# Values first, sums of exps by ones-products, and products of constants in long waits: a change to the start and the first image of a two-layer attention kernel

## The chip, the core and the metric

The kernel runs on one core of one Trainium2 chip. The metric is device time in microseconds (us) of one execution; the profile's times are microseconds from the first instruction, in one profiled execution. The engines are TensorE (PE, matrix products into PSUM), VectorE (DVE), ScalarE (ACT), GpSimd (POOL) and SyncE (SP, which here only starts transfers). Each engine works through its own instructions in the order in which the program wrote them.

## The reference

Input x has 8 images of 256 channels by 32 x 32 positions. Everything is float32. Layer 0, for each image:

```python
q = einsum('bchw,oc->bohw', x, q_w)            # x is group-normalised first
kv = einsum('bchw,oc->bohw', x, kv_w)          # k_map, v_map: 256 channels each
# pooled(t): for sides 32, 16, 11, 5: p = average-pooled t; p = p + depthwise 3x3 convolution of p
ks_ = _layernorm(pooled(k_map).transpose(0, 2, 1), norm_w, norm_b)   # 1024+256+121+25 = 1426 tokens
vs_ = _layernorm(pooled(v_map).transpose(0, 2, 1), norm_w, norm_b)
attn = softmax(einsum('bhqd,bhkd->bhqk', q_g, k) * SCALE)            # 8 heads of 32
out_att = einsum('bhqk,bhkd->bhqd', attn, v)
# a mixing matrix per head from a global token, a projection, and x is added
```

Layer 1 is self-attention over the 1024 positions of each image (one head of 256) and a sum over eight experts of three dense layers, weighted by a gate. The change touches layer 0 alone, its first image most of all.

## The kernel before

**The main loop** (lines 2012 to 2067). Layer 0's attention is cut into units. A unit is one image b, one half c of the heads (four heads), and one half of the queries (512); four units make an image. Keys come in 12 chunks of 128 (the last one smaller, and done for a whole image in one tail step). A step of a unit makes the scores of four heads (`scores`, line 1558: four products into the four-bank PSUM tile `sc`), takes their exp on ACT into a tile `pt` (128 x 2048, six buffers), and, one step later, multiplies them by the values into `pv` (`values`, line 1568). `sc` has one buffer, so the next scores wait for the exp before.

**The sum of the exps.** Two `pt` tiles at a time are added by a transfer that accumulates in memory (`add`, line 1613, on POOL's queue: the trace's pt<-pt). That leaves six pairs a unit. In `sums` (line 1620) DVE adds pairs 1 to 5 to pair 0, in two halves each (the rows pt<-pt,pt), and at the end four products with a 128 x 32 matrix of ones sum pair 0 over the partitions, each into its own 32 columns of the array. `normalise` (line 1639) then divides.

**The background and the planner.** All else (image b+1's keys and values, layer 1 of the images before, weights) is written as Python generators, called threads. `Flow` (line 661) is a planner that runs while the program is built. It keeps a modelled time for each engine and for when each tile is ready (`note`, `cost`, `transfer`), and each thread says what it waits for (`yield pe(tile, tag="sm")`: PE needs this tile and a free small PSUM bank). `step` lets background threads that are ready write their instructions between two steps of the loop, lower rank first, within a budget of PE time; `finish` runs threads until a condition holds. So the order on every engine is fixed when the program is built, by modelled times. Nothing is reordered on the chip by real times.

**PSUM.** Small products share two banks with the tag `sm`, and a third, `sx`, that `small()` (line 944) takes when it is free sooner. In the main loop a plain 128-wide product may be split into four products of 32 columns (`narrow`).

**The start** (before the first step). `prepare(0)` (line 1427) normalises x. `pool_levels` (line 1386) pools x to sides 11 and 5, on POOL and DVE, through a work tile with the tag `pool` that has one buffer; `halve` (line 1137) pools a projected map to side 16 on POOL, through the same tag. `first_maps` (line 1216) projects the four maps of image 0: m = 0, 1 are the two channel halves of the keys, m = 2, 3 those of the values. It writes the large side as two slices of 512 columns, at column 0 and 512, and the small sides as one slice (`HW`). The order is: keys' large slices, values' large slices, then all small ones. ACT copies each slice out and, for values, also writes the centre tap into `acc`. The queries (line 1477, four products of 512 columns for image 0) are a thread of their own with rank 3, next to it.

Keys' large side is convolved on PE with diagonal matrices (`first_keys`, line 1270, in two halves of the image). The values' large side, and all small sides, are convolved on DVE, eight shifted multiply-adds a map and side (`taps`, line 1295; the trace's acc<-map,vec,acc, kn<-ptail and v<-ptail). `first_taps` (line 1309) writes them in this order: values' large side, then the small sides of keys and of values, and it waits until all large slices of all maps are planned. Then `key_tokens` and `value_tokens` transpose to tokens (tiles kt and vt), DVE takes their statistics (tst, tmean, tshift), ACT normalises. They go in three groups of four chunks, so steps 0 to 3, 4 to 7 and 8 to 11 of a unit each need their group.

The next image's `prepare` begins with the load of its x once the four queries of image 0 have been planned (line 1430).

Of the kernel before, what the change touches and what calls it, by code (L numbers as in the profile page):

```python
# [16 lines left out]
P = 128  # L17
C = 256
HW = 1024
HEADS = 8  # L20
DH = 32
# [3 lines left out]
NKC = 12  # L25
# [12 lines left out]
OWN = {"pt", "p1"}  # L38
BUFS = {"sm": 2, "sx": 1}
AHEAD3 = 3  # L40
PACE2 = 8.0
NBOUND = 64
NSTAGED = 64
# [617 lines left out]
class Flow:  # L661
# [4 lines left out]
    class Engine:  # L666
# [3 lines left out]
        def __getattr__(self, op):  # L670
            fn = getattr(self.eng, op)

            def call(*args, **kwargs):
                ins = fn(*args, **kwargs)  # L674
                self.flow.note(self.name, op, ins, args, kwargs)
                return ins

            if op != "matmul":
                return call

            def product(out, lhsT, rhs, **kwargs):
                if not self.flow.narrow(lhsT, rhs):
                    return call(out, lhsT=lhsT, rhs=rhs, **kwargs)
                for j in range(0, P, DH):
                    call(out[j : j + DH], lhsT=lhsT[:, j : j + DH], rhs=rhs, **kwargs)

            return product

    def __init__(self, tc, kit):
        nc = tc.nc  # L690
        self.tc, self.kit = tc, kit
        self.now = dict.fromkeys(("PE", "DVE", "ACT", "POOL", "SP"), 0.0)
        self.last = {}
        self.ready, self.read, self.writer, self.reader, self.slots, self.open = {}, {}, {}, {}, {}, set()
        self.pe = self.Engine(self, "PE", nc.tensor)
        self.ve = self.Engine(self, "DVE", nc.vector)
        self.act = self.Engine(self, "ACT", nc.scalar)
        self.pool = self.Engine(self, "POOL", nc.gpsimd)
        self.sp = self.Engine(self, "SP", nc.sync)
        self.threads = []  # L700
        self.held = set()
        self.cut = {}
        self.also = {}
        self.tiled = None
        self.columns = False
        self.left, self.served = [0.0, 0.0], 0.0
        self.credit, self.port = [0.0, 0.0], 0.0
# [120 lines left out]
    def transfer(self, queue, at, work):  # L828

        span = max(0.0, at - self.served)  # L830
        self.served = max(self.served, at)
        mine, other = queue == "POOL", queue != "POOL"
        left = self.left
        both = 2 * min(left)
        done = min(span, both) / 2
        for i in range(2):
            left[i] = max(0.0, left[i] - done - max(0.0, span - both))
        left[mine] += work
        return 2.2 + left[mine] + min(left[mine], left[other]) + self.served - at

    @staticmethod
    def key(a):
# [85 lines left out]
def attention(tc, kit, f, outer, ended, nb, consts, x, t1, t2, hn, bounds, vecs, q_t, kv_t, proj_t, gqk_t, wqk, wqkv, vecs1, w1_d, w1c, gate_d, wrc, vecs2, bnvec, w2_d, h2d, between, pre, held):  # L928
# [6 lines left out]
    with ExitStack() as ctx:  # L935
# [197 lines left out]
        def source(xp, s0, w):  # L1133
            xi, xl = xp
            return xi[:, :, s0 : s0 + w] if s0 < HW else xl[:, :, s0 - OFFS[2] : s0 - OFFS[2] + w]

        def halve(p, small_p, c, acc):

            yield pool(p[:, :HW])
            pm = p[:, :HW].rearrange("p (h w) -> p h w", h=32)  # L1140
            t2 = T(work, [P, 32, 16], "pool")
            f.pool.tensor_tensor(t2, pm[:, :, 0::2], pm[:, :, 1::2], ALU.add)
            yield pool(t2)
            l2 = small_p.rearrange("p (h w) -> p h w", h=16)
            f.pool.tensor_tensor(l2, t2[:, 0::2, :], t2[:, 1::2, :], ALU.add)
            yield act(small_p)
            f.act.activation(
                acc[:, HW : OFFS[2]],
                small_p,
                AF.Identity,  # L1150
                bias=db(c, 1),
                scale=mid[:, c * 4 + 1 : c * 4 + 2],
            )
            halved.append(acc)
# [61 lines left out]
        def first_maps(xp):  # L1216


            for m in range(4):
                if m < 2:  # L1220
                    p = T(work, [P, 4, 512], "pt", bufs=6).rearrange("p j q -> p (j q)")
                    acc = T(l1, [P, NK], "v") if m else T(work, [P, NK], "kn", bufs=3)
                else:
                    p = pmaps[m - 2]
                    acc = T(work, [P, NK], "acc", bufs=3)
                for t in (p, acc):
                    if t is not p or m < 2:
                        f.split(t, 512, HW)
                first[m] = p, acc
            for m, s0 in [(m, s0) for g in (0, 2) for s0 in (0, 512) for m in (g, g + 1)] + [(m, HW) for m in range(4)]:  # L1230
                if s0 == HW:
                    yield until(lambda: pooled)
                    s0 = OFFS[2]
                w = min(512, NK - s0)
                c = m % 2
                p, acc = first[m]
                src = source(xp, s0, w)
                yield pe(src, tag="sm")
                ps = small()
                for k in range(2):  # L1240
                    f.pe.matmul(
                        ps[:, :w],
                        lhsT=kvw[:, k, m * P : (m + 1) * P],
                        rhs=src[:, k, :],
                        start=k == 0,
                        stop=k == 1,
                    )
                small_levels = s0 > HW and m < 2
                f.act.activation(
                    ptail[:, m, s0 - HW : s0 - HW + w] if small_levels else p[:, s0 : s0 + w], ps[:, :w], AF.Copy  # L1250
                )
                for s, n in enumerate(SIDES):
                    a, z = max(OFFS[s], s0), min(OFFS[s] + n * n, s0 + w)
                    if a < z and (m >= 2 or s):
                        f.act.activation(
                            acc[:, a:z],
                            ps[:, a - s0 : z - s0],
                            AF.Identity,
                            bias=db(c, s),
                            scale=mid[:, c * 4 + s : c * 4 + s + 1],  # L1260
                        )
                if s0 == 512:
                    f.spawn(halve(p, ptail[:, m, :256] if m < 2 else p[:, HW : OFFS[2]], c, acc), 0)
                if (m, s0) == (3, 512):
                    large.append("maps")
                    f.spawn(first_keys(0), 1)
                    f.spawn(first_keys(1), 5)
            whole.append("maps")

# [38 lines left out]

        def first_taps():
            for m in (2, 3):  # L1310
                yield until(lambda: "maps" in large)
                yield from taps(m - 2, 0, *first[m])
                large.append(("values", m))
                read[0] += 1
# [71 lines left out]
        def pool_levels(xi, xl):  # L1386
# [7 lines left out]
            for k in range(2):  # L1394
                one, l3 = img[:, k], level(2)[:, k]

                yield pool(xi)
                t3 = T(work, [P, 32, 11], "pool")
                f.pool.tensor_tensor(t3, one[:, :, 0::3], one[:, :, 1::3], ALU.add)
                yield pool(t3)  # L1400
# [5 lines left out]
                f.pool.tensor_tensor(l3[:, 0:10, :], l3[:, 0:10, :], t3[:, 2::3, :], ALU.add)  # L1406
                yield pool(t3)
                f.pool.tensor_tensor(l3[:, 1:11, :], l3[:, 1:11, :], t3[:, 2::3, :], ALU.add)
                flat = xl[:, k, : OFFS[3] - OFFS[2]]
                f.pool.tensor_tensor(flat, flat, con[:, K_S11 : K_S11 + 121], ALU.mult)  # L1410

            t5 = T(work, [P, 2, 32, 5], "pool")
            ends = [(i * 32 // 5, -(-(i + 1) * 32 // 5)) for i in range(5)]
            for i, (a, e) in enumerate(ends):
# [7 lines left out]
                )  # L1422
            flat = xl[:, :, OFFS[3] - OFFS[2] :]
            f.ve.tensor_tensor(flat, flat, con[:, None, K_S5 : K_S5 + 25].to_broadcast([P, 2, 25]), ALU.mult)
            pooled.append(True)

        def prepare(b):
# [38 lines left out]
            xp = xi, xl  # L1466
            if b == 0:
                todo.extend([None] * 4)
                f.spawn(queries(b, xi), 3)
                yield from first_maps(xp)  # L1470
            else:
                yield from maps(xp)
# [4 lines left out]
        def queries(b, xi):  # L1477

            for c in range(2):
                if b == 0:  # L1480
                    qs[b, c] = T(work, [P, HW], "q", bufs=2)
                for half in range(2):
                    sl = slice(half * 512, half * 512 + 512)
                    q = T(work, [P, 512], "pool") if b else qs[b, c][:, sl]
                    yield pe(xi, q, tag="sm")
                    ps = small()
# [8 lines left out]
                    f.act.activation(q, ps, AF.Copy, scale=vec[:, V_NW + c : V_NW + c + 1])  # L1495
                    if b:
                        f.sp.dma_start(hn[b][:, c, sl], q)
                    else:
                        asked.append((c, half))

# [118 lines left out]

        def sums(n, pairs):  # L1620

            for i in range(1, NKC // 2):
                yield until(lambda: len(pairs) > i)
                for j in range(0, 4, 2):
# [383 lines left out]
        f.spawn(chain(mix(), weights1(), outputs()), 5)  # L2008
        f.spawn(layer1(), 6)
        aside = f.spawn(experts_ahead(), 8)  # L2010
        f.columns = True
        order = [*range(8), NKC - 1, *range(8, NKC - 1)]
        steps = [
            (b, c, half, kc)
# [9 lines left out]
        for i in range(len(steps) + 1):  # L2024
# [40 lines left out]
                    f.act.activation(atts[b1, c1][:, sl1], pv, AF.Copy)  # L2065
            if i < len(steps):
                f.step((PACE, PACE1))
        f.columns = False
        f.finish(lambda: projected[0] == nb)
        f.finish(lambda: aside[1] is None)  # L2070
        f.also.clear()
# [713 lines left out]
```

## Time and profile before

| what | value |
|---|---|
| median of 3 runs | 3241.08 us (3239.82 to 3246.97) |
| the profiled execution's own time | 3241.31 us |
| its span, first to last instruction | 3238.0 us |
| mean granted TensorE clock | 0.983 of full |
| PE busy | 3052.4 us (94%) |
| DVE busy | 2388.8 us (74%) |
| ACT busy | 1631.2 us (50%) |
| POOL busy | 1224.7 us (38%) |
| DVE additions of exps, 128 x 1024 | 320 instructions, 391.7 us, mean 1269 ns |
| exps on ACT, 128 x 2048 | 352 full ones, 660.8 us, mean 1877 ns |
| first exp of the attention | at 80.1 us |
| first exps of units 2, 3, 4 | at 155.3, 204.1, 251.7 us |
| first exp of image 1 | at 295.5 us |

A row of the time-ordered view reads: start, duration of the merged group, engine, line, operation, output<-inputs with sizes, count, and in brackets how long the engine had been idle before and what ended that. All instructions that go through the planner have its one line, L674, so groups are told apart by their tiles. A float32 product shows as two instructions in the trace, so four products are "x8". A row of a stage table gives the stretch, its length, the busy time and count of PE, PE's weight loads, DVE, ACT and POOL, the granted clock, and the share and rate of transfers. In the slices, a digit is a tenth of busy time, and PEclk is the clock that PE was granted.

### The profile page before, as it was taken

To read this page: it belongs to the slowest core of one execution; us is meant where nothing else is said; L and a number is where in the kernel's file an instruction comes from. 1 tells how busy PE (TensorE), PEld (TensorE's weight loads), DVE (VectorE), ACT (ScalarE), POOL (GpSimd) and SP (SyncE) were. 2 spreads that over 40 slices of the span, in tenths; PEclk is the share of its full clock that TensorE was granted. 3 is DMA by queue.
4 is the path that set the end of the run, shared out by engine and by line. 5 is a ranking of instruction groups with operands and counts; after the bars stand their busy time and mean duration, and the time that the engine had idled before them with its cause. 6 is when DMAs were issued, how large, how long until landed. Compare 5 with 4: busy or idle time off the path is not lost.

```text
span 3238.0 us, 57063 instructions
## 1 busy us (share of the span) xinstructions
PE 3052.4 (94%) x22924; PEld 1774.1 (55%) x22924; DVE 2388.8 (74%) x4234; ACT 1631.2 (50%) x2168; POOL 1224.7 (38%) x1309
## 2 busy tenths in 40 slices
PE   8778899899999989989999999999999999999998
PEld 4222234334334333323433357777888888888887
DVE  6786778887988887888654435346878788777776
ACT  4566565566666566566655532334333333444443
POOL 3311413314332232231121121006755566776676
PEclk9899899999999999999999999999999999999999
DMA  1377646655666666656676673124444452000000
GB/s 54 75 163 163 131 98 147 138 135 107 146 143 132 153 130 123 149 121 119 135 190 127 151 220 127 72 91 163 144 152 146 146 173 73 20 20 33 20 14 21
DMA packets 118433, 377.68 MB, mean 117 GB/s; under 512 B 14720, under 2 KB 40648, under 8 KB 94928
## 3 DMA queue, kind: packets, MB, share of 16 engines
q0 software_dynamic: 28608, 179.85, 28.7%
q1 hardware_dynamic: 86048, 192.11, 17.5%
q8 instruction: 183, 3.00, 0.4%
q10 hardware_dynamic: 3504, 1.99, 0.2%
q14 instruction: 90, 0.74, 0.1%
HBM read 120.86 MB, written 87.60 MB: 64 GB/s over the span
## 4 chain that ended last, share of the span: by engine, by line
PE 46%; DVE 3%; issue 2%; DMA 1%; POOL 1%; ACT 1%; DVEq 0%; POOLq 0%; ACTq 0%
PE bank L674 21%; PE y L674 10%; PE sm L674 9%; PE sc L674 2%; PE pv L674 2%; PE sx L674 2%; DVE h L674 1%; DMA pt<-pt 1%; DVE u L674 1%; DVE c L674 1%; ACT pt L674 1%; POOL t L674 0%; DVE t L674 0%; POOL rstd L674 0%; DVE pt L674 0%
## 5 line engine op out<-in xcount | busy, mean ns | idle before, releaser
L674 ACT ACTIVATE pt<-sc 128x2048 f32<-128x2048 f32 x352 | 660.8, 1877 | 322.8 <-PE sc L674 262.9
L674 DVE TENSOR_TENSOR pt<-pt,pt 128x1024 f32<-128x1024 f32 x320 | 391.7, 1269 | 267.6 <-DMA pt<-pt 234.3
L674 DVE SCALAR_TENSOR_TENSOR acc<-map,vec,acc 128x961 f32<-128x961 f32 (+3 forms) x960 | 562.3, 594 | 34.6 <-ACT acc L674 9.3
L674 PE MATMUL sc<-q,kn 32*128 32x512 f32 (+1 forms) x3072 | 426.2, 663 | 101.7 <-ACT pt L674 97.8
L674 PE MATMUL pv<-pt,vt 128*32 128x512 f32 x2816 | 385.9, 621 | 3.6 <-ACT vt L674 3.6
L674 POOL TENSOR_TENSOR rstd<-rstd,mhalf 128x4 f32<-128x4 f32 (+2 forms) x88 | 105.4, 1199 | 719.6 <-DVE rstd L674 586.9
L674 ACT ACTIVATE h<-h,bnvec 128x512 f32<-128x512 f32 x440 | 332.8, 805 | 59.7 <-DVE h L674 50.6
L674 ACT ACTIVATE p1c<-bank 128x256 f32<-128x256 f32 x220 | 84.1, 382 | 549.9 <-PE bank L674 543.7
L674 POOL DMA_DIRECT2D pt<-pt x160 | 146.4, 919 | 435.1 <-ACT pt L674 374.8
L674 DVE TENSOR_TENSOR h<-p1c,bank 128x512 f32<-128x512 f32 x220 | 149.8, 681 | 201.9 <-PE bank L674 194.2
L674 PEld LDWEIGHTS sc<-q,kn 32*128 32x128 f32 (+1 forms) x3072 | 115.1, 181 | 294.1 <-ACT pt L674 188.2
L674 POOL TENSOR_TENSOR tm<-h,tm 128x256 f32<-128x256 f32 x202 | 233.9, 1158 | 15.8
L674 DVE TENSOR_TENSOR h<-u,bank 128x256 f32<-128x256 f32 (+1 forms) x440 | 223.9, 550 | 7.6
L674 PEld LDWEIGHTS pv<-pt,vt 128*32 128x32 f32 x2816 | 56.2, 109 | 281.1 <-issue 261.6
L674 POOL TENSOR_TENSOR tm<-h 128x512 f32<-128x512 f32 x101 | 128.5, 1273 | 195.9 <-ACT h L674 189.5
L674 DVE TENSOR_TENSOR h<-h,gate 128x1024 f32<-128x1024 f32 x128 | 199.4, 1558 | 0.5 <-ACT h L674 0.5
L674 PE MATMUL sm<-y,t 128*32 128x256 f32 (+1 forms) x2432 | 198.2, 379 | 1.1 <-DVE res L674 1.0
L674 PE MATMUL y<-t,s3e 128*128 128x256 f32 x768 | 187.0, 379 | 1.8 <-POOL t L674 1.7
L674 PE MATMUL sm<-p,v 128*32 128x256 f32 (+1 forms) x2064 | 179.5, 385 | 3.9 <-DVE turn L674 3.9
L674 PE MATMUL bank<-t,s1e 128*128 128x256 f32 x714 | 173.8, 379 | 0.2 <-DVE h L674 0.2
L674 POOL TENSOR_TENSOR t<-h 128x512 f32<-128x512 f32 x104 | 132.6, 1275 | 106.7 <-DVE h L674 85.8
L674 POOL TENSOR_TENSOR t<-h,t 128x256 f32<-128x256 f32 x208 | 163.9, 788 | 16.3
(368 smaller groups left out, 5422.3 us busy)
## 6 DMA issues: line engine op xcount, KB each, us to landing
pt<-pt POOLq DMA_DIRECT2D x160, 1024.0 KB, 7.8
h<-h SPq DMA_DIRECT2D x138, 512.0 KB
xi<-in_x_dram SPq DMA_DIRECT2D x16, 512.0 KB
t<-t SPq DMA_DIRECT2D x8, 1024.0 KB
res<-t SPq DMA_DIRECT2D x32, 256.0 KB
t<-res SPq DMA_DIRECT2D x32, 256.0 KB
hn<-res SPq DMA_DIRECT2D x32, 256.0 KB
hn<-hn SPq DMA_DIRECT2D x16, 512.0 KB
```

The source lines that it names most:

```text
L674: ins = fn(*args, **kwargs)
```

## The change

1. **Order of the start.** `first_maps` projects the values' large slices first (map 2, then map 3), then the keys' large slices, then the small slices of all four. `first_taps` waits for each value map by itself. The queries of image 0 become a thread after the last large key slice, beside the first keys' convolution. The users of the one-buffer `pool` tile exclude each other in the plan (`hold`).
2. **Sums of the first four units.** For these, which are image 0, `sums` no longer adds on DVE. It takes bank `sx` at its first pair and sums all six pairs with products of ones, accumulating in PSUM, each pair's buffer being given back after its products. It begins once the unit before has been normalised.
3. **Products of constants.** In the main loop, when the planner sees that a product's operands or its output bank will be ready 1.8 us or more after PE is free, and a small bank is free, it writes products of ones by constants (128 x 128 by 128 x 256) into that bank until the modelled wait is 1.3 us or less. Their results are read by nobody.

```diff
+SUMMED = 4
...
             def product(out, lhsT, rhs, **kwargs):
+                self.flow.warm(out, lhsT, rhs)
                 if not self.flow.narrow(lhsT, rhs):
...
+    def warm(self, out, *srcs):
+
+        if self.keep is None or self.free("sm") > self.now["PE"]:
+            return
+        at = max(self.ready.get(n, 0.0) for a in srcs for n in self.keys(a) if self.writer.get(n) != "PE")
+        for o in self.keys(out):
+            at = max(at, self.read.get(o, 0.0), self.ready.get(o, 0.0) * (self.writer.get(o) != "PE"))
+        if at - self.now["PE"] < 1.8:
+            return
+        bank, self.keep = self.keep, None
+        t = bank()
+        self.open.discard(t.name)
+        while at - self.now["PE"] > 1.3:
+            self.pe.matmul(t[:, :C], lhsT=self.kit.ones, rhs=self.kit.con[:, :C], start=True, stop=True)
+        self.keep = bank
...
+        pooling = []
+
+        def hold():
+
+            yield until(lambda: not pooling)
+            pooling.append(True)
+
         def halve(p, small_p, c, acc):
 
+            yield from hold()
             yield pool(p[:, :HW])
...
-            for m, s0 in [(m, s0) for g in (0, 2) for s0 in (0, 512) for m in (g, g + 1)] + [(m, HW) for m in range(4)]:
+            for m, s0 in [(m, s0) for m in (2, 3) for s0 in (0, 512)] + [
+                (m, s0) for s0 in (0, 512, HW) for m in (range(2) if s0 < HW else range(4))
+            ]:
...
-                if (m, s0) == (3, 512):
-                    large.append("maps")
+                if s0 == 512:
+                    large.append(("map", m))
+                if (m, s0) == (1, 512):
                     f.spawn(first_keys(0), 1)
+                    f.spawn(queries(0, xp[0]), 3)
                     f.spawn(first_keys(1), 5)
...
         def first_taps():
             for m in (2, 3):
-                yield until(lambda: "maps" in large)
+                yield until(lambda: ("map", m) in large)
...
-                f.spawn(queries(b, xi), 3)
                 yield from first_maps(xp)
...
+            if n < SUMMED:
+                yield until(lambda: normalised[0] == n)
+                total = None
+                for i in range(NKC // 2):
+                    yield until(lambda: len(pairs) > i)
+                    yield pe(pairs[i], tag=None if i else "sx")
+                    if i == 0:
+                        total = T(psum, [P, 512], "sx")
+                    for j in range(4):
+                        f.pe.matmul(
+                            total[DH * j : DH * j + DH, :],
+                            lhsT=kit.ones[:, :DH],
+                            rhs=pairs[i][:, j, :],
+                            start=i == 0,
+                            stop=i == NKC // 2 - 1,
+                        )
+                    f.drop(pairs[i])
+                return total
...
-        f.columns = True
+        f.columns, f.keep = True, small
...
-        f.columns = False
+        f.columns, f.keep = False, None
```

`hold` and `pooling.clear()` also stand around each use of the `pool` tile in `pool_levels` and, for later images, in `queries`.

More of the change, by code (lines that the diff above doesn't have):

```diff
@@ L700, in __init__ @@
         self.threads = []
+        self.keep = None
         self.held = set()
@@ L1145, in halve @@
             f.pool.tensor_tensor(l2, t2[:, 0::2, :], t2[:, 1::2, :], ALU.add)
+            pooling.clear()
             yield act(small_p)
@@ L1397, in pool_levels @@
                 yield pool(xi)
+                yield from hold()
                 t3 = T(work, [P, 32, 11], "pool")
@@ L1408, in pool_levels @@
                 f.pool.tensor_tensor(l3[:, 1:11, :], l3[:, 1:11, :], t3[:, 2::3, :], ALU.add)
+                pooling.clear()
                 flat = xl[:, k, : OFFS[3] - OFFS[2]]
                 f.pool.tensor_tensor(flat, flat, con[:, K_S11 : K_S11 + 121], ALU.mult)
+            yield from hold()
             t5 = T(work, [P, 2, 32, 5], "pool")
@@ L1424, in pool_levels @@
             f.ve.tensor_tensor(flat, flat, con[:, None, K_S5 : K_S5 + 25].to_broadcast([P, 2, 25]), ALU.mult)
+            pooling.clear()
             pooled.append(True)
@@ L1483, in queries @@
                     sl = slice(half * 512, half * 512 + 512)
+                    if b:
+                        yield from hold()
                     q = T(work, [P, 512], "pool") if b else qs[b, c][:, sl]
@@ L1497, in queries @@
                         f.sp.dma_start(hn[b][:, c, sl], q)
+                        pooling.clear()
                     else:
```

## The prediction

> **What bounds the kernel now.** I read the page's slices first, then busy time by stage, then each engine in order of time.
>
> ```profile
> PE   8778899899999989989999999999999999999998
> DVE  6786778887988887888654435346878788777776
> PEclk9899899999999999999999999999999999999999
> ```
>
> ```profile
> 76.78:153.76 76.98, 56.34 (x440) 24.12 (x440) 59.39 (x179) 45.16 (x61) 23.26 (x26) 0.83 0.33 71
> 153.76:202.93 49.17, 40.34 (x372) 12.21 (x368) 43.05 (x60) 29.03 (x31) 10.77 (x11) 0.90 0.68 148
> 202.93:249.35 46.42, 37.47 (x341) 13.04 (x337) 38.82 (x83) 35.23 (x43) 11.36 (x14) 1.00 0.72 158
> 249.35:294.29 44.94, 37.36 (x309) 10.69 (x305) 37.89 (x73) 26.82 (x24) 7.00 (x9) 0.96 0.74 180
> 294.29:457.00 162.71, 138.84 (x1280) 47.94 (x1280) 119.90 (x215) 105.98 (x126) 49.75 (x57) 0.95 0.62 128
> 457.00:1000.00 543.00, 508.21 (x5260) 205.96 (x5260) 454.11 (x890) 335.41 (x416) 165.14 (x182) 0.98 0.60 133
> ```
>
> The slices show a TensorE (PE) bound with a weak first eighth. The stage rows (PE, weight loads, DVE, ACT, POOL, granted clock) are, from the second line of numbers on, unit 1 to unit 4 of image 0 (one unit is 11 score steps of four heads and 512 queries), then image 1 to about its third unit, then the middle. PE idles 20.6 us in unit 1, 25.4 us in units 2 to 4 (140.5 - 115.2), 23.9 us in the next row, but only 34.8 us in the 543 us after that. So PE work is the bound from about 460 us on, and what comes before is waiting. A start that comes earlier is kept to the end, because the later work is then done in the same order, only sooner; PE work that is added counts in full unless it falls into idle time.
>
> Who is waited for in unit 1 is read in order of time:
>
> ```profile
> 35.93 19.27 DVE L674 SCALAR_TENSOR_TENSOR acc<-map,vec,acc 128x961 f32<-128x961 f32 x14 [9.27 <-ACT acc L674]
> ...
> 112.19 1.39 DVE L674 BATCH_NORM_STATS2 tst<-kt 128x6 f32<-128x256 f32 x4
> 113.51 2.33 DVE L674 TENSOR_TENSOR pt<-pt,pt 128x1024 f32<-128x1024 f32 x2
> 117.01 1.94 PE L674 MATMUL sx<-p,diag 128*32 128x256 f32 x16 [7.13 <-issue]
> ...
> 146.42 1.94 PE L674 MATMUL pv<-pt,vt 128*32 128x512 f32 x8 [3.55 <-ACT vt L674]
> ```
>
> ```profile
> 86.75 2.09 PE L674 MATMUL sc<-q,kn 32*128 32x512 f32 x8 [2.55 <-ACT pt L674]
> ...
> 90.84 1.14 PE L674 MATMUL sc<-q,kn 32*128 32x512 f32 x8
> ...
> 171.67 1.04 PE L674 MATMUL sm<-pt,con 128*32 128x512 f32 x8
> ```
>
> ```profile
> PE sc L674 <- ACT pt L674: 97.8, 92, 3.1
> ```
>
> DVE starts the value convolution (taps) only at 35.9 us, because the four value slices are the last of the large slices on PE. From there it works nearly without a break, and the third group of key tokens (steps 8 and on) gets its statistics at 112.2, with an addition of exps between statistics and mean. The third group of values is normalised at 147.8. PE stands 7.1 us for the first (its output diag is a copy in the same DVE queue) and 3.6 us for the second. Exps start at 109.0 and then again at 126.5, at 133.9 and again at 155.3. DVE's queue is the limit of unit 1. The next rows serve the costs below: a score product after an idle time and a normal one, and a group of ones-products; the last row sums PE's waits for an exp over the loop (total, times, longest).
>
> **Part 1: values first.** PE starts on the maps at 12.75 either way. Before, queries and keys are ahead of the values: their first copy ends near 31.8. In the new order map 2 is the first product: two slices at the pace of the cold rows (3.78 and 2.82 us for four instructions) end at 19.0, their two ACT passes (0.60 + 0.77 each) at 20.5. The first tap can start there, 15.4 us earlier. DVE's 4.1 us of pooling (2.80 + 1.05 + 0.21), which lay in idle time at 22.5, now comes in between, so the lead is about 11 us. The mutual exclusion of the pooling buffer adds no instruction; its cover is POOL, busy 18.7 of the first 40 us. If it were gone, the small levels would come later by one POOL pass (1.0 + 0.7 us), on nothing before 50 us.
>
> The moved queries carry four products (1.88 us each), four ACT passes (0.69) and no DMA of their own. But image 1's x may be loaded only when all four are asked and x of image 0 has been read: SP's queue issued that load at 36.4, and would now do it near 50. Behind it on SP stand weights first issued at 82.0, so nobody waits; image 1's statistics (57.3) move by a few us and give their place on DVE to image 0's taps. The first keys' convolution can start near 30 instead of 36.2. Queries, 7 us, then fill the wait for key statistics. First score: 44 (two key blocks of 7.4 from 29.5) + 10 to 12 of token work + 0 to 7 of queries = 55 to 63, against 76.8; the second half of the keys (15 us of PE) then follows inside unit 1, so this alone isn't the gain.
>
> **Part 2: ones-products.** Per unit the ten DVE additions go (five pairs, two halves each). Unit mean 1218 ns gives 12.2 us, times four 48.7 us of DVE. Three such pairs (7.1 us) lay before the third value group. With the lead of 11 this puts unit 1's end at 153.8 - 18 = 136 by DVE. By PE: busy 62.4 + 56.3 up to there, less some 8 for a half clock, plus 5 groups of ones (below), plus 12.75 of empty start is 128, and some waits of 10 remain: 138. I take 139, a gain of **15**; bounds 5 (key latency takes DVE's place) and 20.
>
> Each unit gets five more groups of four column products. The group at 171.67 shows 1.04 us, and its successor follows after some 0.88. 20 x 0.88 = 17.6 us of PE. Units 2 to 4 have 15 groups, 13.2 us, against 25.4 us idle there, of which 24.5 us are waits of scores for an exp, mostly of 1.00 us: one group fits into one such wait. A group that is not placed there is paid. I take half: **+6** (0 to +13). On the other side DVE has 36 us less in these 140.5 (busy 119.8), and a pair's buffer is given back by PE after its transfer, without DVE's queue behind it; ACT's exps waited 2.4 us for such a buffer at one place alone. Score waits of 2.7 to 3.1 us occur four times there; most go: **-9** (0 to -15).
>
> Two new waits. The sum starts only when the unit before is normalised; behind it stand pairs in six buffers, and pair 0 no longer stays till the end, so I cost it at nothing; without that cover it is one 3.14 us step a unit. And the sum holds the third small bank (sx) through a unit. In units 2 to 4 that bank carries 13.1 us of products against 28.8 on the other two (sm). I take nothing, since 42 us of products in 140 leave room; up to +6 if half of the 13 slides into the full stage.
>
> Image 1 starts with DVE ahead by 11 + 49 us less what the lead has already been spent on. Of 23.9 us idle in its row some 12 lie at its first keys (1.1 to 2.6 us waits for kt and tshift): **-6** (0 to -12).
>
> **Part 3: products of constants in waits.** No extra instruction where the planner sees no wait of 1.8 us. Their own time is in a wait if the planner is right; one is 0.47 us (the 128x256 product of y: 8 take 1.9). What they could save is the half clock. The granted clock falls short by 0.17 x 77 + 0.10 x 49 + 0.04 x 45 + 0.05 x 163 = 28 us before 457, and by about 24 us in 457 to 1860; with PE busy some 80% of the slow time, the ceiling is 41 us. Here the row and a rule differ. The Trainium skill, "TensorE: Matmul & The Clock Gate", section "HAM oscillation — how this bites in real kernels", says that PE should not idle over about 3.4 us. By it only the five longest idle times of the loop (7.1, 4.7, 3.9, 3.6, 3.6) matter, about 1.7 us each where the clock falls for one 3.4 us window (my estimate from that page): 9 us. The trace shows the score product at 2.09 against 1.14 us after an idle time of 2.55 us, so shorter ones count too, and 1.8 us is a sensible threshold. By rows all of 41 is in reach; but the planner underrates transfers, ACT-bound steps hide part of a slow PE, and image 0's share is partly in the 15 and the 9 above. Between 0 and -25, with +5 if planned waits are not real; I take **-10**, nearer the rule.
>
> **Sum.** -15 + 6 - 9 - 6 - 10 = -34. The profiled execution took 3241.31 us (span 3238.0 and 3.3 around), the median of the runs is 3241.08: no correction. 3241.3 - 34 = 3207.
>
> **Rivals.**
> - *DVE's lead meets another wait.* Before, key tokens had their shift at 58.7 but ACT normalised them at 73.6, behind a PE block. If token latency keeps setting unit 1, only 5 remain of 15, image 1 gains nothing, constants 5, ones and buffers cancel: -10, 3231. For: that wait; against: 7.1 us of PE standing for DVE itself. Chance 0.20.
> - *The ones-products decide (slower).* All 17.6 us land where PE has work, since other products took the waits, the held bank pushes 6 into the full stage, and start and clock give back 10: +14, 3255. It decides once less than about 7 of the 17.6 us fall into waits. For: PE is 94% busy over all; against: 24.5 us of score waits in the very units. Chance 0.10.
> - *Nothing comes of it.* Lead and clock are eaten by image 1's later load and reordering: -2, 3239. Chance 0.08.
> - *As summed:* 3190 to 3224. Chance 0.62.
>
> A difference of 0.2% (6.5 us) is what can be told from none. Faster 0.82 (0.62 + 0.20), same 0.08, slower 0.10. The range goes from 3186 (the sum with a clock gain of 25 and image 1 at its bound) to 3238: it leaves out the slower rival and most of the third.
>
> **What would show it.** Right: first taps near 20 us and no 9.3 us wait before them; unit 2's first exp near 140 instead of 155.3; additions of exps on DVE down from 320 to 280; sx<-pt,con groups within the former 1.00 us waits; granted clock above 0.95 in unit 1; image 1's first exp near 265 to 270 instead of 295.5. Wrong: more idle time before small products in units 1 to 4 (the bank), exps of units 2 to 4 further apart, or a lead at image 1 that has gone by 1000 us.

## The result and the profile after

The changed kernel took 3230.69 us (median of 8 runs, 3222.61 to 3234.16); the kernel before, on the same chips, 3244.1 us (3239.82 to 3247.72). The ratio is 0.9953, 95% interval 0.9944 to 0.9963: 15 us faster by the ratio (13 between the medians), where 34 had been forecast. All later results are such ratios to runs of the kernel before on the same chip, since chips differ by a few us.

The slices of the changed kernel: the clock's dips in the first eighth are gone, and VectorE (DVE) is busier at the start.

```profile
PE   7889799989999999999999999999999999999998
DVE  6973888878888788898544444445887888887776
PEclk9999999999999999999999999999999999999999
```

By stage (columns as before: PE, weight loads, DVE, ACT, POOL, clock, transfers), in its own stretches: unit 1 up to its last exp, then up to unit 4's last exp, image 1 (nearly to its end), then the middle.

```profile
84.60:145.70 61.10, 49.76 (x396) 17.70 (x399) 55.37 (x146) 41.93 (x59) 17.39 (x24) 0.92 0.40 89
145.70:299.90 154.20, 138.22 (x1296) 48.13 (x1288) 90.88 (x226) 101.41 (x119) 39.90 (x42) 0.98 0.68 152
299.90:502.70 202.80, 184.31 (x1800) 64.87 (x1797) 166.62 (x310) 136.18 (x159) 64.60 (x79) 0.99 0.67 142
502.70:1000.00 497.30, 462.51 (x4758) 179.24 (x4760) 423.69 (x800) 308.01 (x373) 143.89 (x158) 0.97 0.61 133
```

Unit 1 has 12 exps, in both kernels, since the tail step stands between its eighth and ninth chunk. So in the kernel before the exps at 155.3, 204.1, 251.7 and 295.5 us, called the first ones of units 2, 3 and 4 and of image 1 above, are the last ones of units 1 to 4. The first ones are at 158.5, 207.3, 254.9 and 302.0.

Unit 1, from its first to its last exp, is shorter by 14 us (61.1 against 75.2), but it starts 4.5 us later. The stretch from there to unit 4's last exp is longer: 154.2 us against 140.2, with 23 us more of PE work. Image 1's first exp is at 303.1 instead of 302.0, so the forecast lead is not there. Image 3's is at 745.2 instead of 775.9, and the last products of attention with values end at 1844.9 instead of 1886.2. From there to the end, though, it takes 1384.9 us instead of 1351.8, with PE busy for 1355.6 instead of 1333.0. Attention was 41 us ahead; the kernel was not.

Over the whole profiled execution, PE's idle time fell from 185.6 to 158.7 us, and what half clock cost within its busy time from 45.9 to 33.8: 39 us together. PE's work, counted at full clock, grew by 31 us, about what the added ones-products and constants take. The 8 us that remain are the difference of the two profiled spans (3238.0 and 3229.8).

Why the start came late is in the changed kernel's order of time, first DVE, then PE.

```profile
20.76 16.00 DVE L675 SCALAR_TENSOR_TENSOR acc<-map,vec,acc 128x961 f32<-128x961 f32 x10 [7.22 <-ACT acc L675]
40.78 2.79 DVE L675 TENSOR_REDUCE pool<-xi 128x64 f32<-128x448 f32 x5 [4.02 <-POOL ptail L675]
...
44.82 7.58 DVE L675 SCALAR_TENSOR_TENSOR acc<-map,vec,acc 128x961 f32<-128x961 f32 x6
```

```profile
47.04 0.33 PE L675 MATMUL sm<-con,acc 128*128 128x128 f32 x1
52.46 1.75 PE L675 MATMUL sm<-con,acc 128*128 128x128 f32 x7 [5.09 <-DVE acc L675]
...
64.06 6.71 PE L675 MATMUL sx<-pt,t 128*128 128x496 f32 x16
...
71.46 6.71 PE L675 MATMUL sm<-pt,t 128*128 128x496 f32 x16
...
79.44 0.82 PE L675 MATMUL sm<-con,kt 128*128 128x128 f32 x3
...
81.44 1.14 PE L675 MATMUL sc<-q,kn 32*128 32x512 f32 x8 [0.25 <-ACT kn L675]
```

The same place in the kernel before:

```profile
56.40 6.71 PE L674 MATMUL sm<-pt,t 128*128 128x496 f32 x16
...
66.31 6.71 PE L674 MATMUL sm<-pt,t 128*128 128x496 f32 x16
...
74.29 0.33 PE L674 MATMUL sm<-con,kt 128*128 128x128 f32 x1 [1.15 <-ACT kt L674]
```

The taps do start at 20.8, as forecast. But DVE's pooling, planned behind ten of them, then waits 4.0 us until POOL has left the one pooling buffer, and six taps wait behind it. The value tokens' transposes had been placed in PE's order by modelled times and stand there 5.1 us for those taps. The second half of the keys' convolution (pt,t at 64 and 71) is again ahead of the first key tokens (con,kt at 79.4), as it was before, and so the first score (sc) comes at 81.4.

PE's waits in units 2 to 4 of the changed kernel (total, times, longest) follow. The waits of scores for exps, 24.5 us before, are nearly gone; the ones-products (sx) wait for their pairs' transfers instead.

```profile
PE sx L675 <- DMA pt<-pt: 7.2, 4, 3.3
PE sc L675 <- ACT pt L675: 5.6, 5, 2.7
```

**A measure that does not mistake order for progress.** I call useful work by time t: PE's busy time up to t, times the granted clock, less the ones-products and products of constants that the kernel before did not have. A product counts from its start to the next one's start, or to its own end if that is earlier; where neighbours' overlap is counted otherwise, a lead moves by up to 3 us. Over a whole execution two plans of the same work also differ by some 6 us in this sum (3006 in the kernel before, 3013 in e7 below), so leads of a few us say little. Before, then the changed kernel:

```profile
0.00:150.00 150.00, 114.99 (x580) 54.00 (x584) 103.15 (x270) 74.19 (x125) 46.95 (x66) 0.91 0.25 64
150.00:300.00 150.00, 123.11 (x1084) 38.67 (x1076) 121.35 (x219) 97.72 (x107) 32.98 (x35) 0.95 0.71 159
```

```profile
0.00:150.00 150.00, 120.45 (x636) 53.99 (x640) 114.54 (x274) 79.97 (x134) 51.18 (x67) 0.94 0.27 68
150.00:300.00 150.00, 134.02 (x1256) 46.95 (x1256) 86.89 (x216) 97.56 (x114) 38.25 (x39) 0.98 0.68 154
```

Before: 0.91 x 115.0 + 0.95 x 123.1 = 221.6. Changed: 0.94 x 120.5 + 0.98 x 134.0 = 244.6, less 22.0 of ones and constants (all products of these two kinds, less what the kernel before has of them) is 222.6. With the clock of each instruction instead of a rounded mean, the changed kernel is 0.8 us ahead at 300 us. It is 13.4 ahead at 500, 2.6 behind at 730, 17.1 ahead at 1840. At 730, when attention was some 31 us ahead, the useful work was the same: other work was as much behind.

### The profile page after: what moved, and what is told of

Read it like the earlier page. It is cut to its first block, busy times and chain, and to the rows that moved or that the text cites. A ratio compares the mean times of both kernels' runs of the same rounds, so it can differ in the third digit from the quotient of the medians.

```text
span 3229.8 us, 57102 instructions
## 1 busy us (share of the span) xinstructions
PE 3071.1 (95%) x22958; PEld 1782.2 (55%) x22958; DVE 2350.0 (73%) x4196; ACT 1628.2 (50%) x2164; POOL 1183.1 (37%) x1273
## 4 chain that ended last, share of the span: by engine, by line
PE 51%; DVE 5%; issue 2%; ACT 1%; POOL 1%; DMA 1%; DVEq 0%; ACTq 0%; POOLq 0%
PE bank L675 21%; PE sm L675 10%; PE y L675 10%; PE sx L675 3%; PE sc L675 3%; PE pv L675 3%; DVE h L675 2%; DMA pt<-pt 1%; ACT pt L675 1%; DVE u L675 1%; DVE pt L675 1%; DVE c L675 1%; POOL t L675 0%; DVE t L675 0%; DVE acc L675 0%
## 5 line engine op out<-in xcount | busy, mean ns | idle before, releaser
L675 DVE TENSOR_TENSOR pt<-pt,pt 128x1024 f32<-128x1024 f32 x280 | 350.7, 1298 | 193.6 <-DMA pt<-pt 177.9
L675 PE MATMUL sc<-q,kn 32*128 32x512 f32 (+1 forms) x3072 | 419.3, 647 | 68.6 <-ACT pt L675 62.2
L675 POOL TENSOR_TENSOR tm<-h,tm 128x256 f32<-128x256 f32 x190 | 217.6, 1145 | 14.9
L675 POOL TENSOR_TENSOR tm<-h 128x512 f32<-128x512 f32 x95 | 121.5, 1279 | 186.0 <-ACT h L675 186.0
L675 PE MATMUL sm<-y,t 128*32 128x256 f32 (+1 forms) x1992 | 182.9, 387 | 3.7 <-DVE res L675 2.5
L675 POOL TENSOR_TENSOR t<-h 128x512 f32<-128x512 f32 x98 | 124.5, 1270 | 132.4 <-DVE h L675 100.1
L675 DVE TENSOR_TENSOR u<-h,bank 128x512 f32<-128x512 f32 x216 | 148.5, 687 | 23.3 <-PE bank L675 0.5
L675 PE MATMUL bank<-h,w2e 128*128 128x256 f32 (+1 forms) x480 | 161.5, 466 | 2.4 <-DVE h L675 2.4
```

## Experiments

All times are medians of 5 to 22 runs. "Useful at 300" is the lead over the kernel before in the measure above, at 300 us.

| run | what | time, us | ratio to before | 95% | useful at 300 |
|---|---|---|---|---|---|
| - | changed kernel | 3230.7 | 0.9953 | 0.9944-0.9963 | +0.8 |
| e1 | order alone | 3264.4 | 1.0058 | 1.0044-1.0072 | -1.6 |
| e2 | sums alone | 3224.2 | 0.9938 | 0.9922-0.9953 | +1.8 |
| e3 | constants alone | 3248.4 | 1.0008 | 1.0000-1.0015 | -0.4 |
| e4 | order, constants | 3267.6 | 1.0061 | 1.0047-1.0074 | -4.4 |
| e5 | order, sums | 3235.8 | 0.9972 | 0.9962-0.9982 | -1.3 |
| e6 | sums, constants | 3222.9 | 0.9932 | 0.9918-0.9947 | +2.2 |
| e7 / e15 | before, 1.70 / 1.68 | 3249.1 / 3260.3 | 1.0011 / 1.0045 | 1.0004-1.0017 / 1.0031-1.0060 | -0.1 / -4.3 |
| e8 / e13 | changed, 1.70 / 1.68 | 3247.1 / 3256.4 | 1.0008 / 1.0034 | 1.0000-1.0015 / 1.0022-1.0046 | -2.1 / +0.2 |
| e11 / e16 | order, 1.70 / 1.68 | 3234.3 / 3235.8 | 0.9961 / 0.9963 | 0.9947-0.9974 / 0.9951-0.9976 | -0.8 / -0.9 |
| e10 / e14 | sums, 1.70 / 1.68 | 3222.9 / 3237.9 | 0.9930 / 0.9971 | 0.9917-0.9944 / 0.9961-0.9981 | +4.2 / +1.1 |
| e9 | changed, scores first | 3249.9 | 1.0015 | 1.0007-1.0023 | -6.3 |
| e12 | sums of 8 units | 3219.7 | 0.9920 | 0.9906-0.9933 | +1.6 |
| e17 | relief alone | 3222.5 | 0.9928 | 0.9916-0.9941 | +15.2 |
| e18 | price alone | 3251.7 | 1.0017 | 1.0011-1.0024 | -2.9 |

### The three parts, alone and in pairs

e1, on the changed kernel:

```diff
-SUMMED = 4
+SUMMED = 0
-        f.columns, f.keep = True, small
+        f.columns = True
```

> Part 1 alone: the new order of the start with its exclusive pooling buffer; sums of exps on VectorE for all units and no products of constants, as before. Theory A (an early start of VectorE is worth its time): about 10 us faster than before, 3234, with the first exp before 80 us. Theory B (the first scores wait for the order of TensorE's own blocks and for the pooling buffer, so the lead is lost before they start): within 5 us of before, 3239 to 3249, with the first exp at 82 to 86 us and VectorE idle some 4 us for GpSimd ahead of its pooling near 37 us.

Neither: 18 us slower, with the first exp at 85.3 and the same 4.0 us wait of DVE for POOL. Theory B was right about the start and wrong about the time. (The nudged plans below take the 18 us back.)

e2 is the kernel before with the new branch of `sums` (`SUMMED = 4`).

> Part 2 alone: the first four units' sums by ones-products, on the kernel before. Theory A (the products fill the waits of scores for exps, and VectorE is relieved): 5 to 10 us faster, 3234 to 3239, with score waits in units 2 to 4 down from 24.5 to under 10 us. Theory B (the products are paid, 17.6 us, since TensorE's work is what ends last): 5 to 15 us slower, 3249 to 3259, with the waits just as small but units 2 to 4 longer.

In time theory A, and more: 20 us faster. PE's waits between 150 and 300 us:

```profile
PE sc L675 <- ACT pt L675: 19.6, 11, 9.8
PE sx L675 <- DMA pt<-pt: 1.8, 3, 1.0
```

Of the waits of scores 19.6 us remain, 9.8 of them in one, where A had them under 10; so the gain isn't just that they are filled.

e3 is the kernel before with `warm`, its call in `product`, and `f.keep = small` in the loop.

> Part 3 alone: products of constants in long planned waits, on the kernel before. Theory A (the half clock after long waits costs what it takes): 6 to 10 us faster, 3234 to 3238, with the time at half clock cut by a third or more. Theory B (the planner fills waits that the chip does not have, or the slow stretches lie in ACT's shadow): within 4 us of before, 3240 to 3248.

Theory B. The longest wait of the kernel before was filled, yet the clock still fell after it. PE's order of time in e3, then PE by stretches of 3 us:

```profile
111.17 4.50 PE L674 MATMUL sm<-con 128*32 128x256 f32 x80
117.28 1.07 PE L674 MATMUL sx<-p,diag 128*32 128x256 f32 x16 [1.60 <-DVE diag L674]
119.16 1.05 PE L674 MATMUL sm<-vec,s 128*128 128x1 f32 x8 [0.81 <-DVE s L674]
120.08 0.72 PE L674 MATMUL sm<-con,kt 128*128 128x128 f32 x4
```

```profile
115.00:118.00 3.00, 1.40 (x32) 0.55 (x20) 2.15 (x9) 0.00 (x0) 1.02 (x2) 1.00 0.00 0
118.00:121.00 3.00, 2.19 (x22) 1.63 (x15) 2.71 (x5) 2.25 (x5) 2.77 (x5) 0.93 0.65 131
121.00:124.00 3.00, 3.00 (x36) 0.86 (x35) 2.75 (x16) 0.84 (x2) 0.00 (x0) 0.50 1.06 216
```

Constants took 4.5 of the 7.1 us. In what follows (1.6 and 0.8 us idle, one-column products, the first 0.5 us of transposes) the clock fell at 120.6 all the same. Of the other long waits, those of 3.6 us (at 142), 3.0 (265), 4.8 (367), 4.1 (458) and 4.0 us (605) are still there: the planner did not foresee them. Over the run, constants took 22 us of PE time, idle time fell by 9 and the loss by half clock by 3.

e4 is the changed kernel with `SUMMED = 0`; e5 is it without `f.keep`; e6 is e2 and e3 together.

> The changed kernel with sums on VectorE for all units (SUMMED = 0): parts 1 and 3. Theory A (the sums carry part of the gain): 5 to 8 us slower than the changed kernel, 3236 to 3239. Theory B (the sums are paid on TensorE and only the rest gains): as fast or up to 8 us faster, 3222 to 3231.

> The changed kernel without products of constants: parts 1 and 2. Theory A (the parts add: order about +18, sums about -22, constants about +2): 3238 to 3244, slower than the changed kernel by 8 to 13 us. Theory B (with the sums on TensorE the constants neither gain nor cost): within 4 us of the changed kernel, 3227 to 3235.

> Parts 2 and 3 on the old order of the start. Theory A (the sums carry all the gain and the new order costs): 3222 to 3228, faster than the changed kernel by 3 to 9 us. Theory B (the new order pays once VectorE no longer adds exps): slower than the changed kernel, 3234 or more.

e4: 35 us slower than the changed kernel by the ratios, not 5 to 8. e5: 5 or 6 us slower than it, between the two theories. e6: theory A. Constants make no difference that can be relied on in any pair (e3: +0.08%, e4 less e1: +0.03%, e6 less e2: -0.06%, changed less e5: -0.19%, the last within what the plans below differ by).

### The plan's own spread

The parts did not add (the order cost 18 us alone, 11 beside the sums). So the planner's model was nudged by 0.6%, which changes what is written when and how products are split into columns, but nothing that is computed:

```diff
-            c = max(0.2, 0.00169 * n)
+            c = max(0.2, 0.00170 * n)
```

and later to 0.00168, for the kernel before, the changed kernel, and the order and the sums alone.

> The kernel before with one number of the planner nudged: its modelled TensorE time per column from 1.69 to 1.70 ns, nothing else. Theory A (a different plan of the same work costs the same): within 5 us of before. Theory B (the planner's choices alone move the time): 8 us or more off, either way; then a part's effect of that size is not the part's own.

> The changed kernel with the same nudge, 1.69 to 1.70 ns. Theory A: within 5 us of the changed kernel, 3226 to 3236. Theory B: 8 us or more off, either way.

> Part 2 alone with the planner's TensorE time per column nudged from 1.69 to 1.70 ns. Theory A (the sums' gain is their own): 3218 to 3232. Theory B (their 22 us were in good part a lucky plan): 3235 or more.

> Part 1 alone with the same nudge, 1.69 to 1.70 ns. Theory A (the new order itself costs about 18 us): 3258 to 3270. Theory B (that cost is the plan's): 3240 to 3255.

> The changed kernel with the planner's TensorE time per column at 1.68 instead of 1.69 ns. Theory A (the changed kernel's plan is of a middling kind): between 3231 and 3247, the two it has shown. Theory B (3231 was its usual time and the nudge up was the exception): 3226 to 3236.

> Part 2 alone, nudged to 1.68 ns. Theory A (the sums' gain is their own): 3218 to 3230. Theory B (two lucky plans): 3235 or more.

> The kernel before, nudged to 1.68 ns. Theory A (its plan hardly moves, as with the nudge up, +4 us): within 6 us of before. Theory B (it has the spread of the others): 10 us or more off, either way.

> Part 1 alone, nudged to 1.68 ns. Theory A (no effect of its own, only the plan's draw): anywhere from 3234 to 3264, with the useful work done by 300 us within 4 us of the kernel before. Theory B (the order costs, and 3234 was luck): 3255 or more. Theory C (the order gains, and 3264 was bad luck): 3238 or less.

The three plans of each, as ratios: before 1.0045, 1.0000, 1.0011 (mean 1.0019); order 0.9963, 1.0058, 0.9961 (0.9994); sums 0.9971, 0.9938, 0.9930 (0.9946); changed 1.0034, 0.9953, 1.0008 (0.9998). Two plans of one kernel differ by up to 0.97%, twice the measured gain. e7 met theory A and e15 theory B. e8 (theory B) lost all of the gain, and e13 missed both of its theories, being slower than before. e11 went from 0.58% slower to 0.39% faster: below both of its ranges, but the cost was the plan's, as theory B had it. e16 fits theory A in its time and its useful work at 300, and theory C in its time as well. e10 held the gain; e14, at 3237.9, missed its range and lies with the theory of luck, but is still faster than all plans of the kernel before.

Only the sums alone stand apart from the kernel before: their slowest plan is faster than its fastest. Further plans on the old order fall on the same sides (e3, without the sums, 1.0008; e6 and e12, with them, 0.9932 and 0.9920). On the new order it is not so: the three plans with sums and constants (0.9998) cannot be told from the three without (0.9994), and under both nudges they are the slower ones, by 0.47 and 0.71%. Order, and the changed kernel as a whole, overlap with the kernel before. The useful work at 300 us moves by at most 4 us under the nudge (last column); most of the spread arises after.

### An early start, forced

e9, on the changed kernel, in `first_keys`:

```diff
+            if half:
+                yield until(lambda: key_parts[0] > 0)
             n = SIDES[0]
```

> The changed kernel, but the second half of the first keys' convolution (15 us of TensorE) is planned only after the first key group is done, so that the first scores come as early as the prediction took them to come. First exp at 58 to 68 us instead of 84.6. Theory A (an early start is kept to the end): 8 us or more faster than the changed kernel, 3223 or less. Theory B (TensorE's useful work by the end of unit 1 is the same, whatever comes first, so the lead is of no worth): within 6 us of the changed kernel, with unit 2's first exp at 135 to 146 us.

Half of B: the lead was of no worth. The time is 0.6% over the changed kernel, which is within that kernel's own three plans (0.9953 to 1.0034); the useful work at 300 us, 6.3 behind, is below all of them (-2.1 to +0.8). PE's order of time in e9:

```profile
67.23 2.09 PE L675 MATMUL sc<-q,kn 32*128 32x512 f32 x8 [0.25 <-ACT kn L675]
...
70.69 6.72 PE L675 MATMUL sm<-pt,t 128*32 128x496 f32 x64
...
84.28 6.73 PE L675 MATMUL sx<-pt,t 128*32 128x496 f32 x64
...
105.47 1.95 PE L675 MATMUL sm<-con,kt 128*128 128x128 f32 x4 [8.26 <-ACT kt L675]
```

The first exp is at 70.5 (58 to 68 expected), 14 us ahead of the changed kernel. The convolution that was put off then stands between the first steps, PE waits 8.3 us for the next key group, and unit 2's first exp is at 158.2, against 151.1 in the changed kernel and the 135 to 146 of theory B.

### What the sums are made of

e17: the kernel before, without DVE's additions of pairs 1 to 5 in the first four units, and without ones-products in their place. These exps are left out of image 0's softmax.

```diff
-                for j in range(0, 4, 2):
+                for j in range(0, 4, 2) if n >= 4 else ():
...
+                if n < 4:
+                    yield ve(pairs[i])
                 f.drop(pairs[i])
```

> The kernel before, with pairs 1 to 5 of the first four units neither added on VectorE nor summed on TensorE: their exps are left out of the sums of image 0's softmax, so the output differs. It shows the relief of VectorE and of the buffers without the ones-products. Theory A (the products are half hidden, as the prediction had it): 6 to 10 us faster than part 2 alone, 3212 to 3218. Theory B (they are paid in full): 15 to 20 us faster than part 2 alone, 3203 to 3209. Theory C (wholly hidden): within 4 us of part 2 alone.

e18: the kernel before, additions kept, and four ones-products for each of these pairs on top, into a small bank; their results are read by nobody.

> The kernel before with VectorE's additions kept, and the ones-products of pairs 1 to 5 of the first four units on top, in the small banks, their result read by nobody: 20 groups, 17.6 us of TensorE. Theory A (half hidden): 6 to 12 us slower than before. Theory B (paid in full): 15 to 20 us slower. Theory C (hidden in the waits of scores): within 5 us of before.

Stretches of e17, then of e18:

```profile
0.00:150.00 150.00, 123.52 (x668) 55.11 (x672) 111.60 (x275) 80.28 (x135) 46.45 (x68) 0.92 0.27 68
150.00:300.00 150.00, 126.39 (x1128) 42.87 (x1120) 91.42 (x227) 106.01 (x120) 45.27 (x53) 0.97 0.76 172
```

```profile
0.00:150.00 150.00, 120.18 (x600) 54.77 (x604) 103.13 (x270) 74.32 (x125) 46.17 (x65) 0.89 0.25 64
150.00:300.00 150.00, 132.26 (x1190) 43.69 (x1182) 127.25 (x232) 96.72 (x108) 30.85 (x34) 0.97 0.71 160
```

By time, both say C or nearly: e17 is as fast as e2, and e18 costs 5.5 us (0.11 to 0.24%) of its 17.6. Up to 300 us they say more. e18 adds 16.6 us of products (at the granted clock), and PE's idle time falls by 14.3: with DVE as slow as before, the waits take most of them. e17 is 15.2 us ahead in useful work at 300, where e2 is 1.8 ahead: with DVE relieved, the ones-products use up nearly all of that relief. The gap of 13.4 us is well over the 4 us by which a nudge moves this measure. That e2 ends as fast as e17 is within the spread of plans, and one plan each can't settle it.

e12 sets `SUMMED = 8` in e2.

> Part 2 alone, but for the first eight units (image 1 too). Theory A (there are waits in image 1 as well, 23.9 us between 294 and 457, and VectorE is as busy): another 5 us or more faster than with four, 3219 or less. Theory B (17.6 us more of ones-products find TensorE at work on layer 1): 5 to 15 us slower than with four, 3229 to 3239.

3219.7 us, the fastest of all, but 4.5 us from e2 and so not told from it: between the theories. By 500 us image 1 had taken 14 us more of ones-products than e2, while PE's idle time was only 6 us less. It is the version to take on these numbers, with the caution of one plan.

## Why the prediction was wrong

The direction was right and the size was not, and even the direction rests on one plan. The main step that failed is the lead by the end of image 0: parts 1 and 2 gave 18 us (15, and 9 less 6), to be kept to the end; it measured 0.8 us of useful work at 300, and image 1's first exp came about 1 us late. The steps, as the prediction put them:

- **"A start that comes earlier is kept to the end, because the later work is then done in the same order, only sooner."** This premise failed too. The order is written by a planner from modelled times, so another start means another order for the 3000 us that follow. Nudges that change nothing computed moved the kernel by up to 0.97%. Where attention did run earlier (image 3 by 31 us), other work was left behind and came due after attention: PE had 22.6 us more to do there. e9's first exp came 14 us earlier, and it had less useful work done by 300 us.
- **"I take 139, a gain of 15" (part 1).** Mis-sized, and the order's share was nothing. Unit 1's last score, which I had put at 153.8 before and 139 after, came at 144.3, a gain of 9.5. PE was idle for 29.5 us up to there, where my sum had 12.75 of empty start and 10 of waits. The taps started at 20.8, as said. But I took the first score at 55 to 63, reckoning PE's blocks by when their data would be ready. It came at 81.4, because the plan put both convolution halves first, and because of two waits that I priced at nothing or not at all: 4.0 us of DVE for the pooling buffer ("if it were gone ... on nothing before 50 us"), and 5.1 us of PE for the late taps. In useful work at 300 us the order alone is 0.8 to 1.6 us behind, in three plans. The rival "DVE's lead meets another wait", with its key tokens behind a PE block, named this and gave 3231; it had 0.20. Its reason held for the start. The agreement in time is chance, since the same kernel nudged gave 3247 and 3256.
- **Ones-products +6, buffers and relief -9.** Waits of scores went from 24.5 to 5.6 us, as said. But the ones-products were not half free beside a relieved DVE: by 300 us, 13.4 us lie between e17 and e2, where I had priced the products at 6. Idle time and half clock together fell by 23 us by then in the changed kernel, and ones and constants took 22 of them. Units 2 to 4, from unit 2's first exp to image 1's, became 8.5 us longer (152.0 against 143.5), not 3 shorter. That the held bank cost little is not shown separately.
- **Image 1, -6.** The waits for image 1's first keys, which I took as some 12 us, add up to 7.8 in the rows of the kernel before. Between 300 and 500 us the changed kernel gained 12.6 us of useful work. The nudged plans of the kernel before gain 8 to 11 in the same stretch, so most of this is that one plan's weakness there.
- **Constants, -10.** Nothing: +0.08% alone. I doubted whether planned waits are real; the main failure was the converse, that most real long waits are not planned ones.
- **The sum.** Of the parts, only the sums have an effect that outlasts the nudge, and that on the old order alone: 0.7% between the means of three plans (1.0019 to 0.9946), over 20 us, where I had given them -3 net and left their relief to be counted under other heads. How those 20 us come about is not shown: at 300 us e2 is only 1.8 us ahead. On the new order, which the changed kernel has, no effect of the sums can be told. The order added nothing that can be told, and the measured 15 us compare the best of three plans with the best of three plans; between the means it is 0.2%.

What stays open: why plans differ after 300 us. Between 500 and 1840 us PE idles 65 us in the changed kernel and 78 and 79 in its nudged plans e8 and e13, which is more than half of the 17 and 24 us of useful work by which they trail at 1840. No single wait is behind it: e8 loses 7.9 us at once, waiting for DVE ahead of 513.6 (image 2's first exp is at 526.5 there and at 510.3 in the changed kernel), but by 600 it trails by only 4 us, and the gap grows again later, with ups and downs. Whether the order costs or gains over many plans can't be said from three, nor whether the sums do on the new order.

## What to carry to other kernels

Where a planner writes the order, measure a change beside a few plans of both kernels (nudge one modelled cost) before a gain of a fraction of a per cent is put down to it. Judge a lead by useful work on the engine that is the bound, not by when a stage starts: an earlier stage can be mere reordering. And before work is moved from a busy helper to the bounding engine "into its waits", ask whether those waits exist once the helper is relieved.

## What the runs showed of the hardware

PE's clock fell in e3 though its idle times near there were 1.6 and 0.8 us: at 120.6, after one-column products and the first transposes, with PE busy 1.4 and then 2.2 of 3 us. The Trainium skill, "TensorE: Matmul & The Clock Gate", section "Part 4: PE-mode transpose", says that transposes do not count as PE work in the same way; as only 0.5 us of them stand ahead of the fall, this stretch does not show it. Idle times of 2.0 to 3.1 us were followed by half clock in some places and not in others: in the kernel before, those of 2.0 us (at 832.8) and 2.6 us (at 84.2) were, those of 2.7 us (at 1218.0) and 3.1 us (at 235.4) were not.
